# Fused attention and non-local block on one core: the order of the row maxima within a step, and GpSimd finishing the softmax sums before the ones-matmul

## The chip, the cores and the metric

The kernel runs on one core of a Trainium2 chip, in one launch. The metric is the device time of that core in microseconds (us); three runs of the kernel before gave a median of 4026.8 us (4026.47 to 4027.5).

## The reference, cut to what matters

The input is x of shape (2, 256, 64, 64), float32: two images, 256 channels, 4096 positions. Two layers follow each other for each image. The first one, in which the change lies, is self-attention with 8 heads of 32 channels over all 4096 positions, a projection, and a residual:

```python
qkv = jnp.einsum('oc,bchw->bohw', w_qkv, x)
q, k, v = jnp.split(qkv, 3, axis=1)
...
scores = jnp.einsum('bhdi,bhdj->bhij', q, k) / jnp.sqrt(jnp.asarray(d, x.dtype))
attn = jax.nn.softmax(scores, axis=-1)
out = jnp.einsum('bhij,bhdj->bhdi', attn, v)
out = out.reshape(b, c, h, w)
return jnp.einsum('oc,bchw->bohw', w_proj, out) + x
```

The second layer is a non-local block (1x1 convolutions, 2x2 max pooling, a softmax over 1024 keys, batch norm and a residual). The change leaves it alone. All work is in float32, but for two small helpers in bfloat16.

## The kernel before, in words

Heads are taken four at a time (a quad), so that attention runs over four pairs of image and quad (`QUAD`, index n). The 4096 queries of each pair are cut into 8 blocks of 512 (index i), and the 4096 keys into 32 tiles of 128 (index j). That makes 32 blocks of 32 steps, one step for each key tile.

Softmax needs the largest score of each query before its first exponential. The kernel therefore computes every score twice. For a block that comes later it makes all scores with the queries on the partitions and reduces them to row maxima (`maxima`, `of_head`); for the block in work it makes the scores again with the keys on the partitions, less the maximum, and takes their exponentials. The maxima work of the later block is woven into the steps by `advance(maxes)`, twice a step.

**One step of a block**, as `attend` emits it at lines 540 to 569:

- *First pair* (heads 0, 1): `score` (L415) makes two score matmuls into the PSUM tile s. `advance(maxes)` then emits two maxima matmuls (`product`, L264) of two other heads. The four run beside each other in the array, as each has 32 rows of it. ScalarE takes the exponential of the pair's 128x1024 scores into p (L551).
- *Second pair* (heads 2, 3): the same with the other heads.
- `weigh` (L439) multiplies the probabilities of the step before with v: four matmuls of 32 output columns each, beside each other, into a scratch tile w. VectorE adds w to `blk.num` (L450).
- `add` (L469, L477) keeps the softmax denominators, as told below.

Each float32 matmul of this kernel is two matmul instructions in the trace, so a group of four makes two passes of four. At every fourth step (j % 4 = 0) the score tile is started anew: `subtract` (L427) first puts minus the maximum into it with a bfloat16 matmul. At the other steps the score matmul adds the difference of two key tiles to what the tile holds, so it has to wait until the exponential of the step before has read it.

**How maxima are made.** Heads 0 and 1 are *plain*: one matmul, and one VectorE reduction of it (`plain`, L276). Heads 2 and 3 are *pairs*: a matmul with the difference of two key chunks goes through a Relu on ScalarE (L283), and one step later a second matmul and the Relu's result are added and reduced in one VectorE instruction (`joint`, L290, followed by a read of its accumulator). Heads 2 and 3 alternate, so that each step has one Relu and one joint. `maxima` sets the order: line 353 gives heads 2, 3 to the first `advance` of a step and heads 0, 1 to the second.

**PSUM scratch.** The four maxima tiles and w of a step come from one pool of four buffers (`ps_m`), taken in turn. So each tile waits for the reader of the tile that was taken four places earlier: with five tiles a step, the fourth maximum of a step takes over the buffer of the w of the step before, and w takes over the buffer of the first maximum of its own step.

**Denominators.** Exponentials of heads 0, 1 go to 128x2x512 tiles (`single`, six buffers), those of heads 2, 3 to tiles that hold two steps (`double`, five buffers). For heads 0, 1 GpSimd adds each tile to the block's first one, `blk.sums[0]` (L469); the last tile (j = 31) is not added but kept in `blk.last`. For heads 2, 3 GpSimd issues, after every odd step from j = 5 on, an accumulating DMA of the whole double tile into `blk.sums[1]` or `blk.sums[2]` in turn (L477). A buffer of the double pool is written again only when the DMA that reads it has landed.

**Normalizing** a block happens during the next one: the generator `normalize` is advanced at j = 2 and at every step from j = 6 (`AFTER`). Its pieces are: at j = 2 a last accumulating DMA, `sums[2]` into `sums[1]` (L483); at j = 6 the matmuls with ones that sum over partitions (L495), in two rounds of four heads (`sums[0]` and the kept last tile for heads 0, 1; the two halves of `sums[1]` for heads 2, 3), and a ScalarE copy of the result (L503); then small DMAs, a reciprocal (L517), and 13 steps later GpSimd's product with `blk.num` into y (L526). The last block of each image is normalized in `project` instead, from four separate sums for heads 2, 3, which makes four rounds.

**Order on the engines.** Each engine runs its queue in order. The queue's order is that of the program, sorted by a scheduler, with `tc.issue_after` holding an instruction behind another: an exponential stands behind the last Relu (`cut`). At the block's turn the projections of q, k, v for later blocks (`make`, L186 and L198) are put in at j = 11, 19 and 27.

Of the kernel before, what the change touches and what calls it, by code (L numbers as in the profile page):

```python
# [12 lines left out]
ALU = mybir.AluOpType  # L13
# [12 lines left out]
NI = N // NB  # L26
NJ = N // P
# [8 lines left out]
def conv_attention(  # L36
# [13 lines left out]
    nc = tc.nc  # L50
# [20 lines left out]
    def scratch(name):  # L71
        return ps_m.tile([P, NB], F32, tag="m", name=name)
# [6 lines left out]
    def double(name):  # L79
        return probs.tile([P, 2, 2, NB], F32, tag="two", name=name, bufs=TWOS)  # L80
# [83 lines left out]
    QUAD = [(b, qd) for b in range(B) for qd in range(QUADS)]  # L164
# [136 lines left out]
    def first_block():  # L301


        for jp in range(NI // 2):
            for g in range(G):
                over = double(f"over_{jp}_{g}").rearrange("p a b n -> p (a b) n")
                for what in range(2):
                    if what == 0:
                        keys = (kd[0] if jp < NI // 4 else last_kd)[:, jp % (NI // 4), :]
                    else:  # L310
                        keys = k[0][:, bass.ts(2 * jp, NB)]
                    s = scores(f"ps_{jp}_{g}_{what}")
                    ps = [
                        product(0, 0, g, h, keys, s[:, h - 2, :] if h >= 2 else None)
                        for h in range(QH)
                    ]
                    for h in range(QH):
                        if what == 0:
                            nc.scalar.activation(over[:, h, :], ps[h], AF.Relu)
                        else:  # L320
                            joint(ps[h], over[:, h, :], g, h, jp)
                    yield
# [23 lines left out]
    def maxima(n, i):  # L346
        if (n, i) == (0, 0):
            yield from first_block()
        else:
            heads = [of_head(n, i, h) for h in range(QH)]  # L350
            for step in range(G * NI):

                for two in ((2, 3) if step % 2 == 0 else (3, 2)), (0, 1):
                    for h in two:
                        next(heads[h])
                    yield
        neg = work.tile([P, NB // P, QH], F32, tag="neg", name=f"neg_{n}_{i}")
        nc.vector.tensor_reduce(neg, part, AX.X, ALU.max, negate=True)
        rows.append(negate(f"{n}_{i}", neg))
        if i == 0 and n > 0:  # L360
            nc.vector.memset(part[:, :, 2:, :], LEAST)
# [26 lines left out]
    def attend(b, y):  # L388
# [63 lines left out]

        DIRECT = 1
        added = None

        def add(blk, j, p, two):
            nonlocal added
            if j == 0:  # L460
                blk.sums[0] = p[0]
            elif j % 2 and (blk.n, blk.i) == (len(QUAD) - 1, NI - 1):

                if j == 1:
                    blk.last.append(p[0])
                else:
                    nc.vector.tensor_add(blk.last[0], blk.last[0], p[0])
            elif j < NJ - DIRECT:
                added = nc.gpsimd.tensor_add(blk.sums[0], blk.sums[0], p[0])  # L469
            else:  # L470
                blk.last.append(p[0])
            if j % 2:
                n = 1 + j // 2 % 2
                if j < 4:
                    blk.sums[n] = two
                else:
                    nc.gpsimd.dma_start(out=blk.sums[n], in_=two, accum_op=ALU.add)  # L477

        def normalize(blk):
            whole = [1, 2]  # L480
            if (blk.qd, blk.i) != (QUADS - 1, NI - 1):
                with tc.issue_after(added.ins):
                    nc.gpsimd.dma_start(out=blk.sums[1], in_=blk.sums[2], accum_op=ALU.add)  # L483
                whole = [1]
                yield
            den = scratch(f"den_{blk.name}")
            mine = [
                [blk.sums[0], *blk.last],
                [blk.sums[n][:, j] for j in range(2) for n in whole],
            ]  # L490
            for n in range(max(map(len, mine))):
                for h in range(QH):
                    those = mine[h // 2]
                    if n < len(those):
                        nc.tensor.matmul(  # L495
                            den[bass.ts(h, D), :],
                            ones[:, :D],
                            those[n][:, h % 2, :],
                            start=(n == 0),
                            stop=(n == len(those) - 1),  # L500
                        )
            r = work.tile([P, NB], F32, tag="r", name=f"r_{blk.name}", bufs=1)
            nc.scalar.copy(r, den)  # L503
            yield
            if (blk.qd, blk.i) == (QUADS - 1, NI - 1):
                nc.vector.reciprocal(r, r)
            else:


                flat = [spare.tile([QH, NB], F32, tag=f"flat{a}", name=f"flat{a}_{blk.name}") for a in range(2)]  # L510
                few = work.tile([P, NB // D], F32, tag="few", name=f"few_{blk.name}")
                nc.sync.dma_start(out=flat[0], in_=r[::D, :])
                nc.sync.dma_start(out=few, in_=flat[0].rearrange("h (c e) -> (h c) e", c=D))
                for _ in range(5):
                    yield
                with tc.issue_after(reduced.ins):
                    nc.vector.reciprocal(few, few)  # L517
                nc.sync.dma_start(out=flat[1].rearrange("h (c e) -> (h c) e", c=D), in_=few)
                for h in range(QH):
                    nc.sync.dma_start(  # L520
                        out=r[bass.ts(h, D), :], in_=flat[1][h : h + 1, :].broadcast_to([D, NB])
                    )
                for _ in range(13):
                    yield
            with tc.issue_after(added.ins):
                nc.gpsimd.tensor_mul(y[:, blk.qd, bass.ts(blk.i, NB)], blk.num, r)  # L526

        waiting, normal = None, iter(())
        for qd in range(QUADS):
            for i in range(NI):  # L530
                blk = Block(qd, i)
                items = [x for x in during(blk.n, i) if x[1] < len(QUAD)]
                both = [None, None]
                for j in range(NJ):
                    if j % 2 == 0:
                        two = double(f"p_{blk.name}_{j}_1")
                    p = [single(f"p_{blk.name}_{j}_0"), two[:, j % 2]]
                    for pair in range(2):
                        if j % 4 == 0:
                            s = both[pair] = scores(f"s_{blk.name}_{j}_{pair}")  # L540
                            subtract(s, pair, blk)
                            advance(maxes)
                            score(s, pair, blk, j)
                        else:
                            s = both[pair]
                            score(s, pair, blk, j)
                            advance(maxes)
                        with ExitStack() as order:
                            if cut is not None:
                                order.enter_context(tc.issue_after(cut.ins))  # L550
                            nc.scalar.activation(p[pair], s, AF.Exp, scale=scale)  # L551
                    if waiting is not None:
                        weigh(*waiting)
                        if j == 0:
                            normal = normalize(waiting[0])
                    add(blk, j, p, two)
                    waiting = blk, j, p
                    if j == 2 or j >= AFTER:
                        advance(normal)
                    if j % 2 == 0:  # L560
                        make_rows()
                        if (i, j) == (0, 2) and blk.n > 0:
                            between(blk.n, 1)
                        if (i, j) == (0, NJ // 4) and blk.n > 0:
                            differences(blk.n, 1, last_kd)
                        if (i, j) == (NI - 1, NJ // 2 + 2) and blk.n + 1 < len(QUAD):
                            between(blk.n + 1, 0)
                    elif j % 8 == 3 and j > 8 and items:
                        advance(make(*items.pop(0)), 9)
# [205 lines left out]


    LEAD = 4
    AFTER = 6
    attending = False


# [77 lines left out]
```

## Time and profile before

| | |
|---|---|
| three runs, median | 4026.8 us |
| the profiled execution's own time | 4027.58 us |
| its span, first to last instruction | 4025.5 us |
| mean granted TensorE clock | 0.997 |
| TensorE matmul busy | 99% of the span |
| VectorE, ScalarE, GpSimd busy | 74%, 66%, 72% |
| mean DMA rate | 141 GB/s |

The profile is of one execution. Its views give the busy time of each engine, groups of instructions (busy time, mean ns of one, and what ended the idle time before them), the waits by pairs of instructions, a chain of work followed back from the last instruction, and a timeline in order of time. Line numbers are those of the kernel before. PE is TensorE's matmuls and PEld its weight loads; DVE is VectorE, ACT ScalarE, POOL GpSimd. Matmuls are pipelined and their ends are modelled, so their starts are read here. A row of the timeline that ends in "x2" or "x4" merges that many instructions, of which the first start is shown.

### The profile page before, as it was taken

To read this page: it belongs to the slowest core of one execution; us is meant where nothing else is said; L and a number is where in the kernel's file an instruction comes from. 1 tells how busy PE (TensorE), PEld (TensorE's weight loads), DVE (VectorE), ACT (ScalarE), POOL (GpSimd) and SP (SyncE) were. 2 spreads that over 40 slices of the span, in tenths; PEclk is the share of its full clock that TensorE was granted. 3 is DMA by queue.
4 is the path that set the end of the run, shared out by engine and by line. 5 is a ranking of instruction groups with operands and counts; after the bars stand their busy time and mean duration, and the time that the engine had idled before them with its cause. 6 is when DMAs were issued, how large, how long until landed. Compare 5 with 4: busy or idle time off the path is not lost.

```text
span 4025.5 us, 72980 instructions
## 1 busy us (share of the span) xinstructions
PE 3993.3 (99%) x28592; PEld 1460.0 (36%) x28592; DVE 2959.7 (74%) x5451; ACT 2668.1 (66%) x3328; POOL 2898.1 (72%) x1851
## 2 busy tenths in 40 slices
PE   9999999999999999999999999999999999999998
PEld 4333333333333333333333333333333333333333
DVE  5877777788777887774457877777888888884444
ACT  4777777777777777751137777777677777777121
POOL 1888888888888888871447888888888888886043
PEclk9999999999999999999999999999999999999999
DMA  1677777877777777880017787877788777778200
GB/s 56 141 163 159 161 165 162 168 162 165 159 161 163 161 161 162 169 199 12 21 35 163 163 167 164 167 161 167 161 167 166 162 162 163 162 161 184 72 16 26
DMA packets 113946, 569.60 MB, mean 141 GB/s; under 512 B 20296, under 2 KB 22600, under 8 KB 52416
## 3 DMA queue, kind: packets, MB, share of 16 engines
q0 software_dynamic: 68832, 501.25, 61.1%
q1 hardware_dynamic: 44080, 62.88, 5.3%
q8 instruction: 224, 3.67, 0.4%
q14 instruction: 122, 1.00, 0.1%
q10 hardware_dynamic: 688, 0.79, 0.1%
HBM read 54.78 MB, written 8.88 MB: 16 GB/s over the span
## 4 chain that ended last, share of the span: by engine, by line
PE 97%; DVE 2%; ACT 0%; POOL 0%; DMA 0%; issue 0%; DVEq 0%; ACTq 0%
PE ps L264 27%; PE w L439 25%; PE s L415 24%; PE y L715 5%; PE s L427 3%; PE v L186 2%; PE q L198 2%; PE k L198 2%; PE den L495 1%; PE proj L584 1%; PE g L640 1%; DVE r L729 1%; PE f L683 1%; PE f L749 1%; PE tp L624 0%; PE tp L620 0%
## 5 line engine op out<-in xcount | busy, mean ns | idle before, releaser
L469 POOL TENSOR_TENSOR p<-p,p 128x1024 f32<-128x1024 f32 x945 | 2293.6, 2427 | 569.9 <-ACT p L551 442.6
L264 PE MATMUL ps<-k,q 32*128 32x512 f32 x6232 | 2115.5, 619 | 2.4 <-DVE part L290 1.0
L551 ACT ACTIVATE p<-s 128x1024 f32<-128x1024 f32 x2048 | 1983.4, 1024 | 106.5 <-PE ps L264 61.2
L276 DVE TENSOR_REDUCE part<-ps 128x1 f32<-128x512 f32 x2136 | 1373.7, 686 | 87.9 <-PE ps L264 57.7
L290 DVE CUSTOM_DVE_ANT_0 ps<-ps,over 128x512 f32<-128x512 f32 x980 | 683.7, 700 | 572.3 <-PE ps L264 410.1
L439 PE MATMUL w<-p,v 128*32 128x512 f32 x8192 | 1092.7, 605 | 0.0
L283 ACT ACTIVATE over<-ps 128x512 f32<-128x512 f32 x916 | 547.2, 597 | 568.6 <-PE ps L264 552.0
L264 PEld LDWEIGHTS ps<-k,q 32*128 32x128 f32 x6232 | 809.7, 184 | 207.6 <-DVE part L276 48.6
L450 DVE TENSOR_TENSOR num<-num,w 128x512 f32<-128x512 f32 x992 | 670.7, 676 | 38.5 <-PE w L439 34.4
L264 PE MATMUL ps<-kd,q 32*128 32x512 f32 x1056 | 568.4, 643 | 1.0 <-POOL kd L219 0.7
L415 PE MATMUL s<-q,k 32*128 32x512 f32 x2048 | 514.6, 593 | 0.0
L415 PE MATMUL s<-q,last_kd 32*128 32x512 f32 x2048 | 510.1, 614 | 0.0
L415 PE MATMUL s<-q,kd 32*128 32x512 f32 x2048 | 509.9, 615 | 0.1
L415 PE MATMUL s<-q,mid_kd 32*128 32x512 f32 x2048 | 509.6, 615 | 0.0
L264 PE MATMUL ps<-last_kd,q 32*128 32x512 f32 x904 | 481.1, 639 | 1.5 <-POOL last_kd L219 1.5
L439 PEld LDWEIGHTS w<-p,v 128*32 128x32 f32 x8192 | 161.5, 108 | 777.4 <-ACT over L283 684.9
L477 POOL DMA_DIRECT2D p<-p x448 | 390.3, 871 | 66.0 <-ACT p L551 65.2
L415 PEld LDWEIGHTS s<-q,mid_kd 32*128 32x128 f32 x2048 | 173.5, 183 | 309.3 <-ACT p L551 306.8
L415 PEld LDWEIGHTS s<-q,kd 32*128 32x128 f32 x2048 | 174.2, 184 | 241.0 <-ACT p L551 215.1
L415 PEld LDWEIGHTS s<-q,last_kd 32*128 32x128 f32 x2048 | 173.5, 183 | 229.6 <-ACT p L551 213.0
L715 PE MATMUL y<-p,kv 128*128 128x512 f32 x512 | 240.0, 608 | 6.4 <-DVE r L729 6.4
L764 ACT ACTIVATE p<-f 128x1024 f32<-128x1024 f32 x64 | 65.5, 1024 | 248.5 <-PE f L749 219.2
(108 smaller groups left out, 2629.5 us busy)
## 6 DMA issues: line engine op xcount, KB each, us to landing
p<-p POOLq DMA_DIRECT2D x478, 1024.0 KB, 7.5
x_k<-in_x_dram SPq DMA_DIRECT2D x32, 512.0 KB
x_q<-in_x_dram SPq DMA_DIRECT2D x30, 512.0 KB
x_res<-in_x_dram SPq DMA_DIRECT2D x16, 512.0 KB
out_dram<-z SPq DMA_DIRECT2D x16, 512.0 KB
r<-flat SPq DMA_DIRECT2D x120, 64.0 KB
x_v<-in_x_dram SPq DMA_DIRECT2D x6, 512.0 KB
wqk_sb<-in_wqk_dram ACTq DMA_DIRECT2D x1, 512.0 KB
```

Of the source, the lines that this page charges most:

```text
L198: nc.tensor.matmul(pq, wqk_sb[:, c, qd, 0 if what == "q" else 1, :], xc[:, c, :], start=(c == 0), stop=(c == NC - 1),)
L264: nc.tensor.matmul(ps, q[n, i][bass.ts(h, D), bass.ts(g, P)], keys[bass.ts(h, D), :], start=True, stop=True,)
L276: reduced = nc.vector.tensor_reduce(part[:, g, h, j : j + 1], ps, AX.X, ALU.max)
L283: cut = nc.scalar.activation(over, ps, AF.Relu)
L290: reduced = nc.vector.tensor_tensor_reduce(out=ps, in0=ps, in1=over, scale=1.0, scalar=LEAST, op0=ALU.add, op1=ALU.max, accum_out=part[:, ...
L415: nc.tensor.matmul(s[:, t, :], kj[bass.ts(h, D), :], q[blk.n, blk.i][bass.ts(h, D), :], start=False, stop=True, skip_group_check=j % 4 > 0,)
L439: nc.tensor.matmul(w[bass.ts(h, D), :], v[blk.n][:, keys(j), h, :], p[h // 2][:, h % 2, :], start=True, stop=True,)
L450: nc.vector.tensor_add(blk.num, blk.num, w)
L469: added = nc.gpsimd.tensor_add(blk.sums[0], blk.sums[0], p[0])
L477: nc.gpsimd.dma_start(out=blk.sums[n], in_=two, accum_op=ALU.add)
L551: nc.scalar.activation(p[pair], s, AF.Exp, scale=scale)
L715: nc.tensor.matmul(acc[i][o], wg[:, 2 * t + j, bass.ts(o, P)], p[:, j, :], **edge)
```

## The change

Five things are edited. (1) The first `advance` of a step gets the plain maxima of heads 0, 1, the second the pairs of heads 2, 3. (2) The score pairs swap places too, so that heads 2, 3 come first: matmuls beside each other still use different rows of the array. (3) GpSimd also adds the exponential of j = 31 of heads 0, 1, placed behind the DMA of that step. (4) GpSimd adds the two halves of `sums[1]`, after the DMA that completes it; one round of ones is then left. (5) `normalize` is advanced at j = 1 (the DMA), j = 4 (the halves) and from j = 7 (the ones). Blocks at the end of an image keep their four rounds for heads 2, 3, and the very last block keeps its sums on VectorE.

```diff
@@ maxima
-                for two in ((2, 3) if step % 2 == 0 else (3, 2)), (0, 1):
+                for two in (0, 1), ((2, 3) if step % 2 == 0 else (3, 2)):
                     for h in two:
                         next(heads[h])
                     yield
@@ add
-        DIRECT = 1
         added = None
...
-            elif j < NJ - DIRECT:
+            elif j < NJ - 1:
                 added = nc.gpsimd.tensor_add(blk.sums[0], blk.sums[0], p[0])
-            else:
-                blk.last.append(p[0])
             if j % 2:
                 n = 1 + j // 2 % 2
                 if j < 4:
                     blk.sums[n] = two
                 else:
-                    nc.gpsimd.dma_start(out=blk.sums[n], in_=two, accum_op=ALU.add)
+                    sent = nc.gpsimd.dma_start(out=blk.sums[n], in_=two, accum_op=ALU.add)
+            if j == NJ - 1 and (blk.n, blk.i) != (len(QUAD) - 1, NI - 1):
+                with tc.issue_after(sent.ins):
+                    added = nc.gpsimd.tensor_add(blk.sums[0], blk.sums[0], p[0])
@@ normalize
-            whole = [1, 2]
+            theirs = [blk.sums[n][:, j] for j in range(2) for n in (1, 2)]
             if (blk.qd, blk.i) != (QUADS - 1, NI - 1):
                 with tc.issue_after(added.ins):
                     nc.gpsimd.dma_start(out=blk.sums[1], in_=blk.sums[2], accum_op=ALU.add)
-                whole = [1]
+                yield
+                theirs = theirs[:1]
+                with tc.issue_after(added.ins):
+                    nc.gpsimd.tensor_add(theirs[0], theirs[0], blk.sums[1][:, 1])
                 yield
             den = scratch(f"den_{blk.name}")
-            mine = [
-                [blk.sums[0], *blk.last],
-                [blk.sums[n][:, j] for j in range(2) for n in whole],
-            ]
+            mine = [[blk.sums[0], *blk.last], theirs]
@@ attend
-                    for pair in range(2):
+                    for pair in (1, 0):
...
-                    if j == 2 or j >= AFTER:
+                    if j in (1, 4) or j >= AFTER:
                         advance(normal)
@@
-    AFTER = 6
+    AFTER = 7
```

On the engines' queues the built program shows the following besides. GpSimd has 61 instructions more. Its halves (L487 of the changed kernel) stand directly behind the addition of j = 4 and directly ahead of the DMA of steps 4 and 5. The DMA of each pair of steps now stands ahead of the addition of its odd step, where before it stood behind it. VectorE's queue goes plain, plain, joint, w instead of joint, plain, plain, w.

## The prediction

> **What bounds the kernel now.** I read the page's busy times and chain of waits first, then the timeline of two ordinary steps, then GpSimd's timeline at the start of a block.
>
> ```profile
> PE 3993.3 (99%) x28592; PEld 1460.0 (36%) x28592; DVE 2959.7 (74%) x5451; ACT 2668.1 (66%) x3328; POOL 2898.1 (72%) x1851
> PE 97%; DVE 2%; ACT 0%; POOL 0%; DMA 0%; issue 0%; DVEq 0%; ACTq 0%
> ```
>
> TensorE sets the end, and no other engine appears in the chain. But 99% hides short waits, so I read the distance between the first score passes of successive steps:
>
> ```profile
> 1001.45 0.70 PE L415 MATMUL s<-q,last_kd 32*128 32x512 f32 x2
> 1001.66 0.68 DVE L450 TENSOR_TENSOR num<-num,w 128x512 f32<-128x512 f32 x1
> ...
> 1002.39 0.21 PEld L264 LDWEIGHTS ps<-k,q 32*128 32x128 f32 x2 [0.20 <-DVE num L450]
> ...
> 1002.82 0.70 DVE L290 CUSTOM_DVE_ANT_0 ps<-ps,over 128x512 f32<-128x512 f32 x1 [0.48 <-PE ps L264]
> ...
> 1003.44 0.16 PEld L439 LDWEIGHTS w<-p,v 128*32 128x32 f32 x8 [0.76 <-ACT over L283]
> ...
> 1003.55 1.29 DVE L276 TENSOR_REDUCE part<-ps 128x1 f32<-128x512 f32 x2
> ...
> 1004.44 0.70 PE L415 MATMUL s<-q,mid_kd 32*128 32x512 f32 x2
> 1004.75 0.68 DVE L450 TENSOR_TENSOR num<-num,w 128x512 f32<-128x512 f32 x1
> ...
> 1005.48 0.29 PEld L264 LDWEIGHTS ps<-k,q 32*128 32x128 f32 x2
> ...
> 1007.53 0.70 PE L415 MATMUL s<-q,last_kd 32*128 32x512 f32 x2
> ```
>
> Steps last 2.99 and 3.09 us. Count from the first score pass (0). The joint starts at 1.37, VectorE's w addition runs from 3.30 to 3.98. The fourth maximum of the next step takes over w's buffer, so its weight load waits for that: at 0.94 in the one step, at 1.04 in the next. What follows is rigid in the trace: w starts 1.05 after that load, the next step 1.00 after w. So the load comes at 4.03 - P (P is the previous step's length), and this step lasts that + 2.05: successive steps sum to 6.08, and alternate about 3.04. With the load by 0.865 a step would last 2.91. Steps with `subtract` last 3.13 and do not wait. 680 steps without `subtract` or projections hold such a wait; their mean is 3.05.
>
> ```profile
> 640.11 2.36 POOL L469 TENSOR_TENSOR p<-p,p 128x1024 f32<-128x1024 f32 x1 [0.61 <-ACT p L551]
> 643.29 2.36 POOL L469 TENSOR_TENSOR p<-p,p 128x1024 f32<-128x1024 f32 x1 [0.83 <-ACT p L551]
> 645.59 0.87 POOL L477 DMA_DIRECT2D p<-p  x1
> ```
> ```profile
> 1283.28 0.88 POOL L477 DMA_DIRECT2D p<-p  x1
> ```
> ```profile
> 1290.50 1.02 ACT L551 ACTIVATE p<-s 128x1024 f32<-128x1024 f32 x1
> 1291.94 1.02 ACT L551 ACTIVATE p<-s 128x1024 f32<-128x1024 f32 x1 [0.43 <-DMA p<-p]
> ```
>
> These are the additions of j = 4 and 5 and the DMA of steps 4 and 5, and, in another block, the same DMA and the exponentials of j = 8. The heads 2, 3 exponential of j = 8 takes over the buffer that this DMA reads. It normally starts 8.12 after the DMA's issue. The landings in 29 blocks took 6.9 to 8.6, mean 7.3: five were late, as this one at 8.58, where the exponential waited.
>
> **The Trainium skill.** "Perfetto Trace Analysis", Identifying the Most-Contended Engine, says that matmul busy time tells little of the distance to the limit; the trace agrees: 99% busy, with 0.08 to 0.18 of wait in a step. The same page, Identifying Dependency Chains, says that an instruction waiting for several engines may have an EventSemaphore ahead of it: the joint (PE and ACT) starts 0.13 after its matmul's signal, plain reductions within 0.02. "GPSIMD Engine Reference", 3.1, gives 4497 ns for an addition of 2048 float32 a partition; the trace has 2427 for 1024, which I use. "TensorE: Matmul & The Clock Gate", Part 3, says that loads overlap matmuls only in other rows of the array; that fits a first pass of 0.54 us against 0.43 for later ones.
>
> **The change, part by part.**
>
> *One round of ones less.* The ones' four passes stretch their step from 1.00 to 2.71 between w and the next score pass (645.51, 648.22), 0.43 a pass. Two passes less are 0.86, in 29 blocks during attention: 25 us, if nothing else fills that place.
>
> *Plain maxima first.* A plain reduction can start at 1.22: in the trace's stretch where all four maxima are plain, the score pass at 893.44 has its first reduction at 894.66. Spacings of before then give 1.22, 1.82 (plains), 2.42 (joint), 3.04 (accumulator), and w's addition 3.15 to 3.83. So w's buffer comes back 0.15 earlier: load at 3.88 - P. But a new wait appears: w now takes the buffer of the first plain, whose reduction ends at 1.91; with signal and load w cannot start before 1.965, so P is at least 2.96. With P = 2.96 the fourth maximum loads at 0.92 and w follows at 1.97: both meet, P is 2.96 to 2.97. ScalarE goes exponential 1.22, Relu 2.12, exponential 2.61 to 3.64, needed at 3.9: hidden by 0.25. Of the 22 such steps of a block, 20 lie outside j = 4 to 8 (below); they average 3.036. One of them waits for ScalarE's first w copy and stays near 3.22; so 60.72 becomes 19 x 2.96 + 3.22 = 59.5: 1.22 a block. 31 blocks have maxima beside them; three of these work on all-plain maxima, VectorE-bound at about 3.2, and gain a fifth: 28.6 x 1.22 = 35 us.
>
> *GpSimd's two additions.* 4.85 us a block. Now it is busy 30 x 2.43 + 15 x 0.87 + 1.28 (L526) + 1.4 (L141 to L145) = 88.6 of 105.66; after, 93.5 of some 104. j = 31's addition falls in the hole of 4.46 idle before the next block's second tile: nothing. The halves are followed by the DMA of steps 4 and 5. Count from the start of step 4: its heads 0, 1 exponential (now second) ends at 3.75, the addition runs 3.9 to 6.25, the halves 6.3 to 8.7, the DMA is issued at 8.65 (before: 8.30). It lands at 15.6 (6.9) or 15.95 (7.3). The heads 2, 3 exponential of j = 8, now the first of its step and behind a shorter road, would start at 3.13 + 3 x 2.96 + 0.86 + 1.33 = 14.2. It waits 1.4 to 1.8. Relu and the other exponential queue behind it, and step 9's second score waits for that one; ScalarE has about 0.3 to spare (a wait of 0.54 in the block above cost 0.12). So step 9 effectively starts at 17.2 to 17.55. Before, steps 4 to 8 took 3.13 + 2.99 + 3.09 + 4.64 + 3.17 = 17.02. With no wait they would take 16.0: the round of ones is bought back here in full, and 0.2 to 0.5 more. At 29 blocks and the mean landing: +15 us.
>
> *Edits costed at nothing.* The DMA at j = 1 stands behind the same number of additions as before; GpSimd idles there, and should the DMA of j = 31 land late (up to 9.2), it would wait under 0.5. The halves' own wait, for that DMA's landing, is over by 2.4. The ones at j = 7 come 2.8 after the halves' end. One buffer of the single pool is freed earlier. The DMAs now ahead of odd additions leave 2.4 earlier outside j = 4 and 5, where nothing waits for them.
>
> Sum: 4027.6 - 35 + 15 = 4007.6 in the profiled execution; the runs' median is 0.8 below it: **4007 us**.
>
> **The rivals.**
> 1. *The DMA lands in time* (an addition starts earlier, or another buffer is free). Then also 1.0 a block is gained: 4027 - 35 - 29 = 3963. Against it: in the built order the exponential of j = 8 still waits for this DMA.
> 2. *The new order of maxima gives nothing*: w behind the first plain waits as long as the fourth maximum did, P stays 3.04. The window of steps 4 to 8 is set by the DMA and still costs 15: 4042. For it: 0.05 of w's start is this wait. Against it: the all-plain stretch shows the reduction at 1.22.
> 3. *Slower, by the DMA queued behind the halves*: its landings are the late sort of before (8.5) in most blocks, or the halves take longer. Each us is a us per block: 17.2 + 1.6 - 17.02 = 1.75, x 29 = 51, - 35: 4043. It turns the sign from a landing of about 8 on. For it: five of 29 were so late; against: 18 were at 6.9.
> 4. *The change does not do what it says*: excluded for the round (60 matmul rows fewer in the built program) and the order of VectorE's queue.
>
> **How the numbers follow.** About 0.2% (8 us) is what this kernel's measurement can tell from no change. My case has 0.54, its own range 3990 to 4022; the first rival 0.14, the second 0.11, the third 0.13; 0.08 for things I do not see, half on each side. Leaving out the tails of the first and third: 3965 to 4040. Faster (under 4019): 0.46 of my case, the first rival, 0.04: 0.64. Within 0.2%: 0.08 of my case, and 0.08 from the edges of the second and third: 0.16. Slower: 0.20.
>
> **What would show it.** Score pass to score pass 2.96 in ordinary steps, VectorE's w addition ending at 3.83, w's load released by a plain reduction (L276). Two ones passes less, 0.86. At each block's j = 8 a ScalarE idle of 1.4 to 1.8 ended by a DMA, the DMA issued 8.65 into step 4, and steps 4 to 8 lasting 17.2 to 17.6. I am wrong if steps stay at 3.04 (order), if that idle is absent (then nearer 3963) or beyond 2.5 (then slower).

## The result, and the profile after

The changed kernel's median is 4016.2 us (4010.9 to 4017.0, 7 runs), that of the kernel before 4026.8 us (4026.5 to 4029.8, 7 runs): a ratio of 0.9968, with a 95% interval of 0.9957 to 0.998. The forecast was 4007 us, between 3965 and 4040. The profiled execution of the changed kernel took 4016.94 us, with a span of 4015.1 us and a granted clock of 0.996.

In the changed kernel the exponential is still L551. GpSimd's additions are L468, its DMAs of two steps L474, the addition of j = 31 is L477, the DMA of `sums[2]` into `sums[1]` L483, the halves L487. First the page of the changed kernel: busy times, then the chain of waits by engine and by line (its shares do not add up to the whole span, so only the order of the entries is read here).

```profile
PE 3945.7 (98%) x28348; PEld 1446.1 (36%) x28348; DVE 2939.2 (73%) x5451; ACT 2671.9 (67%) x3328; POOL 3045.8 (76%) x1912
...
PE 48%; DMA 3%; DVE 2%; ACT 1%; POOL 1%; issue 1%; DVEq 0%; ACTq 0%; POOLq 0%
PE w L439 11%; PE s L415 11%; PE ps L264 11%; PE y L715 5%; DMA p<-p 3%; PE g L640 1%; DVE r L729 1%; PE proj L584 1%; PE f L683 1%; PE s L427 1%; PE f L749 1%; ACT p L551 1%; POOL p L468 1%; PE q L198 1%; PE tp L624 0%
```

TensorE has lost 48 us of busy time, but the run only 11. The chain has a new entry that was at 0% before: a DMA from p to p, one of GpSimd's accumulating DMAs. Next the timeline of an ordinary step, as the prediction showed it for the kernel before:

```profile
999.77 0.70 PE L415 MATMUL s<-q,mid_kd 32*128 32x512 f32 x2
...
1000.99 1.29 DVE L276 TENSOR_REDUCE part<-ps 128x1 f32<-128x512 f32 x2 [0.39 <-PE ps L264]
...
1001.73 0.16 PEld L439 LDWEIGHTS w<-p,v 128*32 128x32 f32 x8 [0.79 <-DVE part L276]
...
1002.19 0.69 DVE L290 CUSTOM_DVE_ANT_0 ps<-ps,over 128x512 f32<-128x512 f32 x1
...
1002.73 0.70 PE L415 MATMUL s<-q,last_kd 32*128 32x512 f32 x2
...
1002.87 0.69 DVE L450 TENSOR_TENSOR num<-num,w 128x512 f32<-128x512 f32 x1
```

The step lasts 2.96 us, from score pass to score pass, where it was 2.99 and 3.09. The plain reductions start at 1.22 and w's weight load comes at 1.96, released by L276: w waits for the first plain maximum, whose buffer it takes over. That is the new limit that the prediction named. Of the 709 intervals from one w to the next that hold only maxima and scores, 583 are 2.96 to within 0.03. The waits by pairs of instructions (us in total, times, longest us) of the changed kernel show this wait and the other one that was forecast:

```profile
PEld w L439 <- DVE part L276: 767.4, 986, 1.2
...
ACT p L551 <- DMA p<-p: 69.2, 29, 4.1
```

Before, the exponential waited for such a DMA 5 times, 2.3 us in all. Now it is 29 times, once in nearly every block and twice in the last. Here is one of them, in GpSimd's and then in ScalarE's timeline:

```profile
742.29 2.37 POOL L468 TENSOR_TENSOR p<-p,p 128x1024 f32<-128x1024 f32 x1 [0.74 <-ACT p L551]
744.62 2.36 POOL L487 TENSOR_TENSOR p<-p 128x1024 f32<-128x1024 f32 x1
746.93 0.84 POOL L474 DMA_DIRECT2D p<-p  x1
747.54 2.62 POOL L468 TENSOR_TENSOR p<-p,p 128x1024 f32<-128x1024 f32 x1
```
```profile
753.83 1.03 ACT L551 ACTIVATE p<-s 128x1024 f32<-128x1024 f32 x1 [1.82 <-DMA p<-p]
```

Step 4 of this block starts at 738.42, with its `subtract`. The DMA of steps 4 and 5 is issued 8.51 us later, behind the halves, and lands after 6.82 us; the exponential of heads 2, 3 at j = 8 starts when it has landed, after 1.82 us of idle.

### The profile page after: what moved, and what is told of

It is laid out like the page before. It is cut to its first block, busy times and chain, and to the rows that moved or that the text cites. A ratio compares the mean times of both kernels' runs of the same rounds, so it can differ in the third digit from the quotient of the medians.

```text
span 4015.1 us, 71903 instructions
## 1 busy us (share of the span) xinstructions
PE 3945.7 (98%) x28348; PEld 1446.1 (36%) x28348; DVE 2939.2 (73%) x5451; ACT 2671.9 (67%) x3328; POOL 3045.8 (76%) x1912
## 4 chain that ended last, share of the span: by engine, by line
PE 48%; DMA 3%; DVE 2%; ACT 1%; POOL 1%; issue 1%; DVEq 0%; ACTq 0%; POOLq 0%
PE w L439 11%; PE s L415 11%; PE ps L264 11%; PE y L715 5%; DMA p<-p 3%; PE g L640 1%; DVE r L729 1%; PE proj L584 1%; PE f L683 1%; PE s L427 1%; PE f L749 1%; ACT p L551 1%; POOL p L468 1%; PE q L198 1%; PE tp L624 0%
## 5 line engine op out<-in xcount | busy, mean ns | idle before, releaser
L468 POOL TENSOR_TENSOR p<-p,p 128x1024 f32<-128x1024 f32 x945 | 2335.1, 2471 | 463.1 <-ACT p L551 455.0
L551 ACT ACTIVATE p<-s 128x1024 f32<-128x1024 f32 x2048 | 2087.0, 1026 | 662.5 <-PE ps L264 396.6
L264 PE MATMUL ps<-k,q 32*128 32x512 f32 x6232 | 2066.3, 628 | 4.0 <-DVE part L276 1.7
L276 DVE TENSOR_REDUCE part<-ps 128x1 f32<-128x512 f32 x2136 | 1369.9, 686 | 578.0 <-PE ps L264 562.7
L450 DVE TENSOR_TENSOR num<-num,w 128x512 f32<-128x512 f32 x992 | 679.9, 685 | 103.6 <-PE w L439 101.5
L264 PEld LDWEIGHTS ps<-k,q 32*128 32x128 f32 x6232 | 642.7, 183 | 60.8 <-DVE part L276 9.5
L415 PE MATMUL s<-q,kd 32*128 32x512 f32 x2048 | 523.6, 621 | 32.4 <-ACT p L551 32.3
L264 PE MATMUL ps<-kd,q 32*128 32x512 f32 x1056 | 520.0, 597 | 0.7 <-POOL kd L219 0.7
L264 PE MATMUL ps<-last_kd,q 32*128 32x512 f32 x904 | 437.4, 590 | 1.5 <-POOL last_kd L219 1.5
L474 POOL DMA_DIRECT2D p<-p x448 | 389.3, 869 | 3.6 <-issue 1.8
```

The lines of the kernel that those rows point to most:

```text
L264: nc.tensor.matmul(ps, q[n, i][bass.ts(h, D), bass.ts(g, P)], keys[bass.ts(h, D), :], start=True, stop=True,)
L276: reduced = nc.vector.tensor_reduce(part[:, g, h, j : j + 1], ps, AX.X, ALU.max)
L415: nc.tensor.matmul(s[:, t, :], kj[bass.ts(h, D), :], q[blk.n, blk.i][bass.ts(h, D), :], start=False, stop=True, skip_group_check=j % 4 > 0,)
L450: nc.vector.tensor_add(blk.num, blk.num, w)
L474: sent = nc.gpsimd.dma_start(out=blk.sums[n], in_=two, accum_op=ALU.add)
```

## The experiments

The experiments were timed in two sets beside the kernel before, whose median was 4027.2 us in both. Ratios are to it, with their 95% intervals. The row of the change is the result above, beside 4026.8 us.

| kernel | us, median | ratio |
|---|---|---|
| the change | 4016.2 | 0.9968 (0.9957 to 0.998) |
| e1: new order alone | 3987.1 | 0.9902 (0.9885 to 0.9918) |
| e2: new sums alone | 4071.9 | 1.0113 (1.0097 to 1.0128) |
| e3: the change, halves behind the DMA | 3968.0 | 0.9853 (0.9838 to 0.9867) |
| e4: the change without the halves | 3988.7 | 0.9904 (0.9889 to 0.9919) |
| e5: the change, halves half as wide | 3978.2 | 0.9878 (0.9863 to 0.9893) |
| e6: e3 with the old order | 4006.4 | 0.9948 (0.9935 to 0.996) |
| e7: e3 with another last block | 3965.9 | 0.9845 (0.9832 to 0.9859) |

The theory (A) was that of the prediction: both halves of the change save what was forecast, and the DMA of steps 4 and 5, issued late because GpSimd does the halves first, takes it back. Its rivals were that the order of the maxima gives little (B), and that it is GpSimd's additional work as such that costs (C).

**e1: the order alone.** The kernel before, with two lines of the change:

```diff
-                for two in ((2, 3) if step % 2 == 0 else (3, 2)), (0, 1):
+                for two in (0, 1), ((2, 3) if step % 2 == 0 else (3, 2)):
...
-                    for pair in range(2):
+                    for pair in (1, 0):
```

> The kernel before with only the order changed (plain maxima and heads 2, 3 first); the sums and both rounds of ones stay. Theory A (order gains some 35 us, the sums lose most of their 25 us to the DMA of steps 4 and 5): ordinary steps of 2.96 us, no idle of ScalarE at j = 8, 3988 us (3980 to 3996). Theory B (the change's gain is the round of ones, the order is worth little): within 8 us of 4027.

Measured: 3987.1 us (3986.6 to 3989.6). The two lines alone save 40 us. They are worth more than the whole change, so the rest of the change costs 29. Rival B falls.

**e2: the sums alone.** The changed kernel with those two lines put back.

> The change with the order put back (pairs and heads 0, 1 first); GpSimd's two additions and one round of ones stay. Theory A: here the DMA of steps 4 and 5 stands behind the halves and the addition of j = 5, is issued about 10 us into step 4, and the exponential of j = 8 waits about 1.2 us; the 0.86 us saved are given back: 4030 us (4020 to 4040). Theory B: the round is saved, 4002 to 4018 us.

Measured: 4071.9 us (4067.7 to 4079.0), 42 us more than A's value and outside both theories. GpSimd's timeline of e2 shows a part of the reason:

```profile
430.87 2.36 POOL L468 TENSOR_TENSOR p<-p,p 128x1024 f32<-128x1024 f32 x1 [0.61 <-ACT p L551]
433.20 2.35 POOL L487 TENSOR_TENSOR p<-p 128x1024 f32<-128x1024 f32 x1
435.52 2.36 POOL L468 TENSOR_TENSOR p<-p,p 128x1024 f32<-128x1024 f32 x1
437.82 0.84 POOL L474 DMA_DIRECT2D p<-p  x1
```
```profile
446.92 1.02 ACT L551 ACTIVATE p<-s 128x1024 f32<-128x1024 f32 x1 [3.14 <-DMA p<-p]
```

With the old order the DMA stands behind the addition of j = 5 too, and leaves 9.78 into step 4. I had counted that. What I had not counted is how long it takes to land: above 8.0 us in 11 of 29 blocks (seven of them at 9.0, as this one), against 5 of 29 in the changed kernel. An ordinary block with a landing of 6.9 lasts 105.5 to 106.2, about what it did before (105.65); one with 9.0 lasts 107.7 to 109.9. The longest, 110.7, had a landing of 7.6, but L483's own DMA took 9.05 there, and the halves wait for that. L483 itself waits for an earlier landing nine times, 19.0 us in all, where the prediction had allowed under 0.5 for a wait.

The late landing also has a sequel for which the forecast has no term. In eight blocks of e2 and in the last one, the profile shows a granted TensorE clock of 0.50 for 3.4 or 6.8 us, directly after the wait. Here is TensorE in the block shown above, and then the row of busy times of one stretch (its third number from the end is the granted clock):

```profile
448.00 0.70 PE L415 MATMUL s<-q,kd 32*128 32x512 f32 x2 [2.62 <-ACT p L551]
...
449.21 1.94 PE L439 MATMUL w<-p,v 128*32 128x512 f32 x8
451.08 1.22 PE L415 MATMUL s<-q,mid_kd 32*128 32x512 f32 x2
...
453.57 1.06 PE L439 MATMUL w<-p,v 128*32 128x512 f32 x8
454.57 0.70 PE L415 MATMUL s<-q,kd 32*128 32x512 f32 x2
```
```profile
448.90:452.30 3.40, 3.40 (x20) 0.93 (x20) 1.98 (x3) 1.42 (x2) 2.81 (x2) 0.50 0.25 46
```

From w to the next score pass it takes 1.87 us in that stretch and 1.00 in the step after. Two ordinary blocks with landings of 9.07 and 9.06 last 107.65 us without such a stretch and 109.28 with one. The mean granted clock of this execution was 0.992, against 0.997 before; if TensorE had work in all of that time, this is worth some 20 us (an estimate, 0.005 of the span of 4077 us). Whether the late landing, with this sequel, is the whole cause was open at this point; e6 shows that the surplus goes with the DMA's place.

**e3: the halves behind the DMA.** The changed kernel, in which GpSimd issues the DMA of steps 4 and 5 first, then adds the halves, then j = 5.

```diff
+            if j == 5:
+                sent = nc.gpsimd.dma_start(out=blk.sums[1], in_=two, accum_op=ALU.add)
+                advance(normal)
...
-                with tc.issue_after(added.ins):
-                    nc.gpsimd.tensor_add(theirs[0], theirs[0], blk.sums[1][:, 1])
+                with tc.issue_after(sent.ins):
+                    added = nc.gpsimd.tensor_add(theirs[0], theirs[0], blk.sums[1][:, 1])
...
```

> The change with one swap on GpSimd: the DMA of steps 4 and 5, then the halves, then the addition of j = 5. All its work stays. Theory A: the DMA leaves 6.2 us into step 4 and lands before the exponential of j = 8 needs its buffer, except for the late landings: 3965 us (3955 to 3978). Theory C (GpSimd's load as a whole, two more additions a block, is what takes the gain): it stays at 4005 to 4018 us.

Measured: 3968.0 us (3965.9 to 3969.9). The same additions, the same DMAs and the same matmuls, with two instructions exchanged on GpSimd, save 48 us. Theory C falls. GpSimd's and ScalarE's timelines of the same block as above (here L460 is that DMA, L494 the halves, L474 the additions, L558 the exponential):

```profile
734.46 2.36 POOL L474 TENSOR_TENSOR p<-p,p 128x1024 f32<-128x1024 f32 x1 [0.76 <-ACT p L558]
736.77 0.86 POOL L460 DMA_DIRECT2D p<-p  x1
737.38 2.65 POOL L494 TENSOR_TENSOR p<-p 128x1024 f32<-128x1024 f32 x1
739.71 5.07 POOL L474 TENSOR_TENSOR p<-p,p 128x1024 f32<-128x1024 f32 x2
```
```profile
744.76 1.03 ACT L558 ACTIVATE p<-s 128x1024 f32<-128x1024 f32 x1 [0.57 <-PE s L415]
```

Step 4 starts at 730.60, so the DMA leaves at 6.17 instead of 8.51. The exponential's idle is now ended by its own scores, after 0.57 us. So of the 1.82 above, 1.25 was the wait for the DMA. Two additions now merge behind the halves: GpSimd catches up only later, and the exponentials wait for its additions only 0.3 us in the whole run.

**e4: no halves.** The changed kernel with the halves' addition left out and two rounds of ones again; j = 31 is still added by GpSimd.

```diff
-                theirs = theirs[:1]
-                with tc.issue_after(added.ins):
-                    nc.gpsimd.tensor_add(theirs[0], theirs[0], blk.sums[1][:, 1])
+                theirs = theirs[::2]
```

> The change without the halves' addition: the ones have two rounds again, the second for heads 2, 3 alone; GpSimd still adds j = 31. Theory A: no wait at j = 8, the second round costs its 0.86 us: 3988 us (3980 to 3998), as with the order alone; so the addition of j = 31 costs nothing. Theory C: half the load, halfway: about 4000 us.

Measured: 3988.7 us (3987.2 to 3989.7), as e1 but for 1.6 us: the addition of j = 31, which e1 does not have, costs nothing that can be seen. An ordinary block lasts 104.25 in e4 and 103.39 in e3: the round of ones is worth 0.86, the forecast figure.

**e5: halves half as wide.** The addition is shortened, so that the DMA leaves earlier while all else stays in its place.

```diff
-                    nc.gpsimd.tensor_add(theirs[0], theirs[0], blk.sums[1][:, 1])
+                    nc.gpsimd.tensor_add(theirs[0][:, 0], theirs[0][:, 0], blk.sums[1][:, 1, 0])
```

> The changed kernel with the halves' addition made only half as wide (128x512, head 2's); it leaves head 3's second half out of its denominator. That addition is then some 1.2 us shorter, so that GpSimd issues the DMA of steps 4 and 5 some 7.5 us into step 4 instead of 8.6. Theory A (the exponential of heads 2 and 3 at j = 8 waits for that DMA's landing, because GpSimd issues it late): the landings of 6.8 to 6.9 us come in time and cost nothing, only those that last longer still cost something: 3980, between 3972 and 3990, some 36 us below the changed kernel for an addition that nothing reads early. Theory B (what costs is GpSimd's work as such[...]): half of one addition less of some twelve in a block gives a few us: 4005 to 4014.

Measured: 3978.2 us (3977.5 to 3978.8). In the traces most blocks with a landing of 6.8 to 7.1 have the length of e3 (103.4 to 103.6), so 1.1 us less work for GpSimd brought 1 us a block, as a DMA that leaves 1.1 us earlier should. This run shortens the work and moves the DMA at once; it is e3, with all of the work, that tells the two apart. ScalarE's idle there is down to this:

```profile
746.07 1.02 ACT L551 ACTIVATE p<-s 128x1024 f32<-128x1024 f32 x1 [0.73 <-DMA p<-p]
```

**e6: the old order, halves behind.** The fourth corner of order and DMA: e3 with the two lines of e1 put back.

> The changed kernel with the old order of maxima and of pairs, and with the halves' addition moved behind the DMA of steps 4 and 5. It fills the fourth corner: both orders, each with the DMA early and late. Theory A: the DMA leaves some 6.8 us into step 4, nothing waits for its landing, and what is left of the change is the one round of ones saved, 0.86 us in some 29 blocks: 4002, between 3996 and 4012. If the sums cost time with the old order for another reason than the landing (the same work of GpSimd, some other wait), as the run with both orders put back, at 4071.87, leaves possible: 4020 or more.

Measured: 4006.4 us (4005.4 to 4007.5). Exponentials wait for such a DMA only three times any more, 1.0 us in all (28 times and 58.2 us in e2). So e2's surplus was no cost of the old order: moving the DMA ahead of the halves (and here of the addition of j = 5 too) saves 65 us there, and 48 with the new order. The halved clock is gone from the eight blocks too. And with the DMA in time the two parts add up to within 2 us: order alone -40, sums alone -21, together -59 (e3).

**e7: another last block.** e3, and in the very last block the old order of pairs, and no halves for the block before it (two rounds of ones there).

```diff
-                    for pair in (1, 0):
+                    for pair in (0, 1) if (blk.n, i) == (len(QUAD) - 1, NI - 1) else (1, 0):
...
+                if (blk.n, blk.i) == (len(QUAD) - 1, NI - 2):
+                    theirs = theirs[::2]
...
```

> The changed kernel with the halves' addition moved behind the DMA of steps 4 and 5, and in the very last block, where no maxima lie beside the scores, pairs in the old order and no halves for the block before it (two rounds of ones there). Theory A: that block lasted 82.51 us with the halves moved, 79.23 in the kernel before; two or three us of that come back: 3965, between 3960 and 3970. If the last block's excess has another cause than the order and the halves: 3968, as without this edit.

Measured: 3965.9 us (3963.0 to 3966.5). From its first w to its last that block lasted 82.52 us in the trace, against 85.04 in e3 and 82.74 in the kernel before. (The 79.23 of the expectation ends one w earlier than its 82.51; over the same stretch the kernel before has 80.11.) Of the two edits the halves are the larger part: e6, with the old order and the halves, has 85.07 there, and e4, with the new order and no halves, 83.93. The ranges of e3 and e7 overlap a little, and their intervals for the most part: the runs alone do not tell 2 us apart. Either of the two beats both kernels of the case by 48 us or more.

## Why the prediction was right, and where it was 9 us off

- *Plain maxima first, 1.22 a block, 35 us.* Right, down to the new wait and the 2.96. e1 measured 40; its steps 4 to 8 gain too, as its DMA is not held up, which the sum for the whole change had set aside.
- *One round of ones, 0.86 a block, 25 us.* Right: 0.86 between e4 and e3.
- *Two additions on GpSimd.* j = 31: nothing, as forecast. Halves: the DMA was to leave 8.65 into step 4 and left at 8.51; the wait was to be 1.4 to 1.8 and is 1.25 with the shortest landing. Without a wait steps 4 to 8 were to take 16.0: in e3 it is 16.00, from the start of step 4 (its `subtract`) to step 9's first score pass. With it they were to take 17.2 to 17.55. In the changed kernel from the w issued in step 4 to that in step 9 it takes 16.83 with a landing of 6.82, in e3 15.83, so the wait costs 1.00 there and the stretch counts 17.00. The longer landings cost more, up to 2.7 (a block with 8.56 lasts 106.13, in e3 103.39). Between e3 and the changed kernel the two traces differ by 42.5 us over the 31 blocks ahead of the last: the prediction's sum has 29 x (17.02 + 0.52 - 16.0) = 44.7 for it, with its 15 us / 29 = 0.52. It had taken the mean landing of before, 7.3, for a DMA that is issued at another place; that it came out at 7.4 was in part luck, as e2, with 7.7 in the mean, shows.
- *The step that failed: 29 blocks alike.* The sum was 4027.6 - 35 + 15, a gain of 20. From the first w of the run to the first w of the very last block the traces show a gain of 21.1. The very last block went from 82.74 to 89.49 us, from its first w to its last, and for it the sum has no term; nor has it one for what stands behind that block, which went from 293.9 to 297.5. No maxima lie beside the last block's scores, so its steps are 2.3 to 2.9 and the DMA's 7 us span more of them. The halves' own wait, which the prediction had over by 2.4, and the DMA at j = 1, which was to wait under 0.5, both hold GpSimd up there. GpSimd's and ScalarE's timelines of the changed kernel:

```profile
3635.02 0.87 POOL L483 DMA_DIRECT2D p<-p  x1 [4.73 <-DMA p<-p]
3635.63 5.38 POOL L468 TENSOR_TENSOR p<-p,p 128x1024 f32<-128x1024 f32 x2
3641.97 2.35 POOL L487 TENSOR_TENSOR p<-p 128x1024 f32<-128x1024 f32 x1 [0.96 <-DMA p<-p]
3644.27 0.86 POOL L474 DMA_DIRECT2D p<-p  x1
```
```profile
3651.68 1.94 ACT L551 ACTIVATE p<-s 128x1024 f32<-128x1024 f32 x2 [4.07 <-DMA p<-p]
```

L483 waits 4.73 us for the landing of an earlier DMA. The halves then wait 0.96 for L483's, the DMA of steps 4 and 5 waits behind the halves, and ScalarE stands idle 4.07 us. TensorE has nothing to do for 3.60 us of this, and then the granted clock is 0.50 for 6.8 us, which can cost up to half of that (an estimate). One such stretch of 3.4 us stands in the block before, which went from 97.34 to 99.15 us, and one behind the last block; before, there were none at these places. In e7 the same DMA (L490 there) waits just as long, but with no halves to follow the block is back at 82.52, and none of its exponentials from there on waits for a DMA:

```profile
3591.56 0.87 POOL L490 DMA_DIRECT2D p<-p  x1 [4.75 <-DMA p<-p]
3592.17 5.09 POOL L474 TENSOR_TENSOR p<-p,p 128x1024 f32<-128x1024 f32 x2
3597.22 0.86 POOL L460 DMA_DIRECT2D p<-p  x1
```

The last block's 6.7 us and the 3.6 behind it are what the 4007 lacks. The 3.6 are the less certain part: in the nine traces what stands behind the last block lasts 293.1 to 298.2 us, and how much of it belongs to the change is not shown.

- *All-plain blocks.* They were to gain a fifth of 1.22. Two of them grew by 1.1 and 1.2 us instead (108.64 to 109.78, 108.63 to 109.83). With the halves behind the DMA they shrank to 107.14. So it is the same wait, and there it costs 2.7 against some 1.5 in the mean of the blocks. The plain maxima are not the reason: the landings of these two blocks, 8.45 and 8.53, were among the five late ones, and the ordinary block with 8.56 lost 2.7 as well.
- *The rivals.* The first, a DMA in time, was priced at 3963: that is e3, at 3968. The second, no gain by the order, is refuted by e1. The third, late landings, did not come in the changed kernel (5 of 29 above 8.0; the kernel before has 4 of these 29, not the five that the prediction counted), but it is a part of what happened in e2, which ended on the slow side.

Open: why a landing takes 6.8 to 7.0 us in one block and 9.0 in another. It is not chance alone: four of the changed kernel's five late ones come in pairs at the same place of the two images (the 6th and 22nd block, the 8th and 24th). In the trace of the changed kernel each landing above 7.0 has a packet of an instruction queue within the transfer's window, and those below 7.0 have none that starts in it; but in many of them that packet begins only some 7.0 after the issue, when a short transfer would have landed, so it may accompany the delay and not make it. Giving the exponentials another buffer in place of moving the DMA was not tried.

## What to carry to other kernels

When work is given to an idle engine, look at what stands behind it in that engine's queue: 2.4 us of additions that nothing was waiting for yet delayed a DMA issue, and the DMA's landing freed a buffer on the critical path. Issue the transfer first and do the work in its shadow; that exchange was worth 48 us here, more than four times what the whole change had brought. And before multiplying a cost by the number of blocks, look at the first, the last and the odd ones separately: what hides a wait in the ordinary block may be missing there.

## What was not expected of the hardware

- The landing of the same 1 MB accumulating DMA, from issue, scatters in one run: in the changed kernel 13 of 29 took under 7.0 us, 11 took 7.0 to 8.0, and 5 took 8.3 to 8.6; in e2 seven took 9.0. Where the exponentials wait for it, the time of a run scatters as well (4010.9 to 4017.0, and 4067.7 to 4079.0 in e2); with the DMA in time it is 3965.9 to 3969.9 in e3 and 4005.4 to 4007.5 in e6.
- After some waits the granted TensorE clock is 0.50 for 3.4 or 6.8 us, so that the wait costs more than its own length. In e2 TensorE stood idle for 2.6 us or more in ten places of the attention blocks, and such a stretch follows nine of them; the four idle times of 2.05 to 2.19 us in the changed kernel have none behind them, but one of 1.95 has. What decides was not found. The four runs of e2 are ordered by it: 4067.7, 4068.8, 4074.9 and 4079.0 us at mean clocks of 0.995, 0.994, 0.993 and 0.992.
